# Pinning the making of convolution weights and the stores of zeros to the steps that call them

## The chip, the core and the metric

One NeuronCore of a Trainium2 chip runs the whole program; the other seven are not used. The metric is device time in microseconds for one execution, over a batch of 8 images of 256 channels and 64 x 64 pixels, all in float32. Five engines work side by side, each through a queue of its own: TensorE (PE, matrix products into PSUM), VectorE (DVE), ScalarE (ACT), GpSimd (POOL) and SyncE (SP), which here issues every DMA of the program. Engines wait for each other through semaphores.

## The reference

Two layers follow each other. Cut to what matters:

```python
# layer 0: attention with a reduced set of keys
xr = layernorm_over_channels(conv(x, w_sr, stride=4))        # 16 x 16 positions
q, (k, v) = w_q @ x, split(w_kv @ xr)                        # 8 heads of 32
x = x + gamma_s * (w_out @ (softmax(q @ k.T / sqrt(32)) @ v))
# layer 1: linear attention over two scales
qkv = w_qkv @ x                                              # 768 channels
agg = grouped_1x1(depthwise_5x5(qkv, w_dw), w_pw)            # groups of 8
ms  = concat([qkv, agg])                                     # heads of 8: relu(q), relu(k), v
att = relu_q @ (relu_k.T @ [v, 1]);  att = att[:-1] / (att[-1] + 1e-15)
out = x + batchnorm(w_proj @ att)
```

The kernel multiplies the depthwise 5 x 5 filter and the grouped 1 x 1 filter into one set of weights, so that `agg` becomes a product on TensorE. Making these combined weights is work that depends on no image.

## The kernel before, in words

The program has three passes, one after the other. (A fourth function, `general`, stands behind a test at the end and is not run on these inputs.) Between the passes the data go through scratch memory in HBM.

**First pass** (`first_pass`). Layer 0 and the first projection of layer 1. The main loop runs over n = 0 to 256 + 15. Each n is one step: image b = n // 32, and within the image a strip of 512 pixels (8), a half of the channels (2) and a half of the keys (2). A step issues four products of scores (L784) into PSUM banks, four exponentials on ScalarE (L790), and for the step before it the values (`valued`, L808). At every second step the sums are added on GpSimd (`joined`, L819), the denominators are made (`counted`, L824), and VectorE turns and inverts them (`normed`: L836, L837, L839, L841). Every fourth step, n mod 4 = 2, the output projection (`added`, L856) and the residual sum on VectorE (L857) end a strip, and SP stores it (L860). After every second strip `differences` (L871 to L874) prepares a 2 x 2 scheme of seven products for q, k and v (`qkv`), and these 21 products (L900) are given out over the next seven steps. VectorE and ScalarE empty their banks (L913, L916, L962, L969, L973, L982), and VectorE turns the results (L920) for the stores into `planes` (L933), `k` (L943) and `v` (L948). Scores, projections and products share five PSUM banks in turn. In steps 12 to 19 of an image the strided convolution for the next image runs (`keys_values`, L697), for which SP loads the weights `wsr` (L694) in four buffers; its layer norm follows in steps 20 to 23.

Two jobs without a deadline of their own run beside this loop:

- `conv_weights`, a generator over four parts j = 2, 3, 0, 1 with eight pieces each. It loads `wd` (L668), adds (L670), and for each piece multiplies two broadcast operands on VectorE into `wb` (L674) and stores `wb` to HBM (`wt`, L680). `wd` and `wb` have one buffer each, so a product waits until the store of the product before it has landed. The loop takes one piece per call:

```python
if n > 32 and n % 8 in (3, 6):
    next(weights, None)
if n < n_all:
    b, at = n // 32, n % 32
    if at == (20 if b == 0 else 2):
        border(b)
```

- `border`, which fills the rim of the padded `v` of one image with zeros from the tile `nil`: four stores for each image (L661, L662).

What is written in the loop at some n does not have to run there. The layer that builds the program keeps data dependences and then orders each engine's stream by its own estimate of when operands are ready. An instruction with early operands can move far ahead in its engine's stream. `tc.keep_in_program_order(ins)` adds one constraint: `ins` stays behind the instruction of the same engine that was written just before it. It adds no wait.

**Second pass** (`second_pass`). 64 units of (group of channels, head group, image). It loads `wt`, `planes`, `k` and `v`, makes the combined convolution on TensorE (`convolve`, L1231 and L1235), sums keys with values (L1257, L1274), applies the sums to the queries (`applied`, L1348) and stores attention outputs to `att` (`stored`, called for unit r - 1 in a loop that runs to r = 63, and for the last unit behind the loop). Its constants `taps`, `mix`, `msk`, `rep_w`, `pix` and `ones` are loaded or filled as early as memory of the first pass is free.

**Third pass** (`third_pass`). Reads `att` and `planes`, applies the sums, projects (L1585), normalises and adds the residual.

Of the kernel before, what the change touches and what calls it, by code (L numbers as in the profile page):

```python
# [29 lines left out]
ALU = mybir.AluOpType  # L30
AX = mybir.AxisListType

P = 128
# [5 lines left out]
NB2 = 2 * NB  # L39
NK = NB * NB  # L40
HEADS = 8
D0 = C // HEADS
D1 = 8
# [531 lines left out]
def first_pass(ctx: ExitStack, tc: tile.TileContext, a, fine, planes, x2d, kd, vd, wtd):  # L575
    nc = tc.nc
# [21 lines left out]
    consts, x_tiles = {}, {}  # L598
# [58 lines left out]
    def border(b):  # L657
        v = vd[b].rearrange("n y x e -> y x n e")
        src = nil.rearrange("p (n e) -> p n e", n=8)
        for i in (0, NB2 + 1):  # L660
            nc.sync.dma_start(v[i], src)  # L661
            nc.sync.dma_start(v[1 : NB2 + 1, i], src[:NB2])  # L662


    def conv_weights():
        for j in (2, 3, 0, 1):
            wd = made.tile([P, 16, 6, 16], F32, tag="wd", name=f"wd_{j}", bufs=1)
            nc.sync.dma_start(wd[:, :, :4], a.w_big[:, j].rearrange("p g (n f) -> p g n f", n=4))  # L668

            nc.vector.tensor_add(wd[:, :, 4:], wd[:, :, 0:4:2], wd[:, :, 1:4:2])  # L670
            for i in range(8):
                w = made.tile([P, 2, 6 * 16, D1], F32, tag="wb", name=f"wb_{j}_{i}", bufs=1)
                gs = slice(2 * i, 2 * i + 2)
                nc.vector.tensor_tensor(  # L674
                    w,
                    wd[:, gs].rearrange("p g n f -> p g (n f)").unsqueeze(3).to_broadcast([P, 2, 6 * 16, D1]),
                    consts["wsmall"][:, j, gs].unsqueeze(2).to_broadcast([P, 2, 6 * 16, D1]),
                    ALU.mult,
                )
                nc.sync.dma_start(wtd[j][:, gs], w.rearrange("p g n o -> p g (n o)"))  # L680
                yield
# [309 lines left out]


    weights = conv_weights()
    new_x(0)
    ahead = keys_values(0)
# [29 lines left out]
    n_all = len(order)  # L1025
    todo = {}
    for n in range(n_all + 16):
        m = n - 1
        if n < n_all:
            b, s, c, kc = order[n]  # L1030
# [24 lines left out]
        if n >= 6 and (n - 6) % 4 == 0 and (n - 6) // 4 < B * NG:  # L1055
            b, s = (n - 6) // 4 // NG, (n - 6) // 4 % NG
# [11 lines left out]
# [4 lines that stand above are left out]
            if b + 1 < B:  # L1072
                if at == 10 and b > 0:
                    load_x(b + 1)
                if at == 12:
                    ahead = keys_values(b + 1)
                if 12 <= at < 20:
                    next(ahead)
                    next(ahead)
                elif at >= 20:  # L1080
                    next(ahead, None)
# [20 lines left out]
def second_pass(ctx: ExitStack, tc: tile.TileContext, a, planes, kd, vd, wtd, kvd, attd):  # L1102
    nc = tc.nc
# [21 lines left out]
    n_all = len(units)  # L1125
# [76 lines left out]
    kts, reds, raws, mraws, state, few, qs, bds, done = {}, {}, {}, {}, {}, {}, {}, {}, {}  # L1202
# [161 lines left out]
    def stored(u, par):  # L1364
        t, k, b = units[u]
        c0 = P * t + D0 * k
        tc.keep_in_program_order(
            nc.sync.dma_start(attd[b][c0 : c0 + D0, par].rearrange("c j n -> j c n"), done.pop((u, par)))
        )

    positive(0)
    paired(0, 1)
    for u in range(n_all + 3):
        p, q, r = u - 1, u - 2, u - 3
# [9 lines left out]
        if r > 0:  # L1384
            stored(r - 1, 0)
            stored(r - 1, 1)
# [37 lines left out]
        if now and u + B < n_all:  # L1424
            b = units[u][2]
            load_weights(u + B - b, 1 if b < 4 else 0, b % 4)
    stored(n_all - 1, 0)
    stored(n_all - 1, 1)

# [350 lines left out]
```

## Time and profile before

| | us |
|---|---|
| median of 3 runs (3954.38 to 3956.75) | 3954.98 |
| the profiled execution | 3955.74 |
| its span, first to last instruction | 3954.0 |
| granted TensorE clock over the span | 0.991 |
| VectorE busy in each of the images 2 to 6 of the first pass, which take 248.2 each | 142.5 to 142.8 |

The page gives busy shares over the whole span. The kernel's three passes have different limits: up to some 2010 us the first pass, up to some 3297 us the second, then the third. The forty slices show them as steps in weight loads and GpSimd:

```profile
PEld 4433434435344343443346888888888885555555
DVE  2567565564655646556674566666666664444443
POOL 2334343343433434334433344444444440000000
PEclk9999999999999999999999999999999999999999
DMA  7655544353543534444549887878878757777774
```

Each digit is a tenth of a slice of 99 us. TensorE loads weights for most of the second pass, GpSimd is silent in the third, and DMA engines are busiest in the first two slices and in the second pass. SP issues all transfers in one queue; the ones that the change touches are these (count, size each):

```profile
wt<-wb SPq DMA_DIRECT2D x32, 768.0 KB
...
v<-nil SPq DMA_DIRECT2D x16, 136.0 KB
v<-nil SPq DMA_DIRECT2D x16, 128.0 KB
wd<-in_w_big_dram SPq DMA_DIRECT2D x4, 512.0 KB
```

### The profile page before, as it was taken

Reading aid. Unit: us, or ns where it says so; the run is one execution under the profiler, and the core shown is the slowest. Engines: PE = TensorE matmul, PEld = TensorE weight load, DVE = VectorE, ACT = ScalarE, POOL = GpSimd, SP = SyncE. Lnnn points to the kernel's source line nnn. Section 1 sums busy time; section 2 is a strip of 40 time slices with the busy share of each in tenths; the row PEclk is TensorE's granted clock in tenths of the full one; section 3 lists DMA queues with packets and bytes.
Section 4 is the critical chain, followed back from the end, with each engine's and each line's share of the span. In section 5 each row is a group of like instructions: output and inputs, shape, how many; then the busy total and the mean of one; then the engine's idle time right before and its main releaser. Section 6 shows DMA issues by size and latency. Waiting matters only on the chain. (4 is left out here: it accounts for less than half of the span.)

```text
span 3954.0 us, 70041 instructions
## 1 busy us (share of the span) xinstructions
PE 3873.1 (98%) x27074; PEld 2276.1 (58%) x27074; DVE 2266.0 (57%) x3752; ACT 1516.9 (38%) x3473; POOL 1300.0 (33%) x1394
## 2 busy tenths in 40 slices
PE   8999999999999999999998999999999998999998
PEld 4433434435344343443346888888888885555555
DVE  2567565564655646556674566666666664444443
ACT  3344344443444434444432222222222223554444
POOL 2334343343433434334433344444444440000000
PEclk9999999999999999999999999999999999999999
DMA  7655544353543534444549887878878757777774
GB/s 233 198 152 173 161 137 127 95 155 102 138 129 96 153 100 133 132 117 116 135 116 267 245 233 221 231 223 226 229 214 231 208 145 193 224 210 223 205 227 141
DMA packets 570039, 691.35 MB, mean 175 GB/s; under 512 B 60128, under 2 KB 429280, under 8 KB 565600
## 3 DMA queue, kind: packets, MB, share of 16 engines
q1 hardware_dynamic: 569696, 686.78, 61.2%
q8 instruction: 215, 3.52, 0.4%
q14 instruction: 128, 1.05, 0.1%
HBM read 412.54 MB, written 274.10 MB: 174 GB/s over the span
## 5 line engine op out<-in xcount | busy, mean ns | idle before, releaser
L819 POOL TENSOR_TENSOR e<-e,e 128x512 f32<-128x512 f32 x512 | 685.0, 1369 | 925.7 <-PE av L808 873.2
L790 ACT ACTIVATE e<-sc 128x512 f32<-128x512 f32 x1024 | 530.3, 602 | 801.4 <-PE sc L784 794.4
L1231 PE MATMUL cv<-w,c 128*128 128x128 f32 x3072 | 387.7, 280 | 5.6 <-POOL c L1171 5.1
L1231 PEld LDWEIGHTS cv<-w,c 128*128 128x128 f32 x3072 | 361.2, 193 | 36.2 <-issue 29.3
L784 PE MATMUL sc<-q,kk 32*128 32x512 f32 x2048 | 316.7, 640 | 6.5 <-DVE whole L916 4.8
L1603 DVE TENSOR_TENSOR y<-z,xs 128x256 f32<-128x256 f32 x256 | 141.9, 638 | 310.8 <-ACT z L1594 287.3
L900 PE MATMUL qkv<-differences,combined 128*128 128x512 f32 x576 | 306.2, 623 | 0.4 <-DVE differences L872 0.2
L1274 PE MATMUL sums<-vq,r 128*32 128x288 f32 x4096 | 304.9, 410 | 0.8 <-issue 0.7
L1248 ACT ACTIVATE r<-s 128x512 f32<-128x512 f32 x256 | 160.9, 629 | 316.7 <-DVE s L1247 311.7
L808 PE MATMUL av<-e,vv 128*32 128x512 f32 x2048 | 275.3, 610 | 3.1 <-ACT att L828 3.1
L916 DVE TENSOR_TENSOR whole<-part,qkv 128x512 f32<-128x512 f32 x256 | 175.3, 687 | 178.6 <-PE qkv L900 166.9
L1594 ACT ACTIVATE z<-p,bn 128x256 f32<-128x256 f32 x256 | 133.6, 577 | 313.1 <-PE p L1585 207.4
L1235 PE MATMUL cv<-c,w 128*128 128x128 f32 x2048 | 253.3, 277 | 0.0
L1585 PE MATMUL p<-att,wproj 128*128 128x512 f32 x512 | 249.4, 609 | 1.2 <-ACT att L1568 1.2
L769 PE MATMUL q<-x,wq 128*128 128x512 f32 x512 | 244.3, 599 | 0.0
L1585 PE MATMUL p<-agg,wproj 128*128 128x512 f32 x512 | 240.6, 592 | 0.0
L697 PE MATMUL sr<-x,wsr 128*128 128x256 f32 x1024 | 232.7, 381 | 8.1 <-DMA wsr<-in_w_sr_dram 8.1
L1235 PEld LDWEIGHTS cv<-c,w 128*128 128x128 f32 x2048 | 239.7, 192 | 0.0
L856 PE MATMUL o<-att,wout 128*128 128x512 f32 x512 | 232.8, 596 | 6.2 <-DVE att L841 6.2
L697 PEld LDWEIGHTS sr<-x,wsr 128*128 128x128 f32 x1024 | 195.4, 191 | 59.7 <-issue 26.8
L1238 ACT COPY both<-cv 128x512 f32<-128x512 f32 x128 | 74.9, 585 | 402.9 <-PE cv L1231 351.0
L1247 DVE TENSOR_TENSOR s<-cv,both 128x512 f32<-128x512 f32 x256 | 171.8, 672 | 87.2 <-PE cv L1235 45.5
(143 smaller groups left out, 6029.7 us busy)
## 6 DMA issues: line engine op xcount, KB each, us to landing
vq<-v SPq DMA_DIRECT2D x256, 384.0 KB
planes<-stage SPq DMA_DIRECT2D x128, 578.0 KB
d<-planes SPq DMA_DIRECT2D x128, 578.0 KB
raw<-planes SPq DMA_DIRECT2D x128, 272.0 KB
x<-in_xp_dram SPq DMA_DIRECT2D x64, 512.0 KB
wsr<-in_w_sr_dram SPq DMA_DIRECT2D x128, 256.0 KB
x<-x SPq DMA_DIRECT2D x128, 256.0 KB
k<-turned SPq DMA_DIRECT2D x256, 128.0 KB
```

The costliest lines, as they stand in the source:

```text
L697: nc.tensor.matmul(ps[:, oc], w[:, ci, oc * P : (oc + 1) * P], strips(b, f // 2)[:, ci, f % 2 * NK : (f % 2 + 1) * NK], start=(f == ci == ...
L769: nc.tensor.matmul(ps, consts["wq"][:, ci, c * P : (c + 1) * P], strips(b, s)[:, ci], start=(ci == 0), stop=(ci == 1),)
L784: nc.tensor.matmul(scs[h], kks[b][rows, c, kc * P : (kc + 1) * P], qs[rows], start=True, stop=True)
L790: nc.scalar.activation(e, scs[h], AF.Exp, scale=D0**-0.5)
L808: nc.tensor.matmul(sums["av"][cols], vvs[b][:, kc, c * P + h * D0 : c * P + (h + 1) * D0], es[h], start=(kc == 0), stop=(kc == 1),)
L819: nc.gpsimd.tensor_tensor(es1[h], es0[h], es1[h], ALU.add)
L856: nc.tensor.matmul(ps, consts["wout"][:, c, oc * P : (oc + 1) * P], att[c], start=(c == 0), stop=(c == 1))
L900: nc.tensor.matmul(ps, w, x, start=True, stop=True)
L1231: nc.tensor.matmul(out, x, m, start=(da == 0), stop=(da == 1))
L1235: nc.tensor.matmul(out, m, x, start=(da == 0), stop=(da == 1))
L1274: nc.tensor.matmul(ps[h * D0 : (h + 1) * D0, : 36 * D1].rearrange("p (r n e) -> p r n e", r=3, e=D1), kt[:, par, h, 2 * r + c], vq[:, r : ...
L1585: nc.tensor.matmul(ps.rearrange("p (f q n) -> p f q n", f=4, q=4), wproj[:, j, oc * P : (oc + 1) * P], src, start=(j == 0), stop=(j == 3),)
```

## The change

Three places get or lose the constraint of program order. The two stores of `border` get it on SP. The sum for `wd` and the products for `wb` get it on VectorE; their loads and stores stay free. The stores of attention outputs, which all had it, lose it for the last three units.

```diff
@@ border
         for i in (0, NB2 + 1):
-            nc.sync.dma_start(v[i], src)
-            nc.sync.dma_start(v[1 : NB2 + 1, i], src[:NB2])
+            tc.keep_in_program_order(nc.sync.dma_start(v[i], src))
+            tc.keep_in_program_order(nc.sync.dma_start(v[1 : NB2 + 1, i], src[:NB2]))
@@ conv_weights
-            nc.vector.tensor_add(wd[:, :, 4:], wd[:, :, 0:4:2], wd[:, :, 1:4:2])
+            tc.keep_in_program_order(nc.vector.tensor_add(wd[:, :, 4:], wd[:, :, 0:4:2], wd[:, :, 1:4:2]))
             for i in range(8):
...
-                nc.vector.tensor_tensor(
-                    w,
...
-                    ALU.mult,
+                tc.keep_in_program_order(
+                    nc.vector.tensor_tensor(
+                        w,
...
+                        ALU.mult,
+                    )
                 )
                 nc.sync.dma_start(wtd[j][:, gs], w.rearrange("p g n o -> p g (n o)"))
                 yield
@@ stored
-        tc.keep_in_program_order(
-            nc.sync.dma_start(attd[b][c0 : c0 + D0, par].rearrange("c j n -> j c n"), done.pop((u, par)))
-        )
+        put = nc.sync.dma_start(attd[b][c0 : c0 + D0, par].rearrange("c j n -> j c n"), done.pop((u, par)))
+
+        if u < n_all - 3:
+            tc.keep_in_program_order(put)
```

No operation is added or removed, and no operand changes.

More of the change, by code (lines that the diff above doesn't have):

```diff
@@ L673, in conv_weights @@
                 gs = slice(2 * i, 2 * i + 2)
-                nc.vector.tensor_tensor(
-                    w,
-                    wd[:, gs].rearrange("p g n f -> p g (n f)").unsqueeze(3).to_broadcast([P, 2, 6 * 16, D1]),
-                    consts["wsmall"][:, j, gs].unsqueeze(2).to_broadcast([P, 2, 6 * 16, D1]),
-                    ALU.mult,
+                tc.keep_in_program_order(
+                    nc.vector.tensor_tensor(
+                        w,
+                        wd[:, gs].rearrange("p g n f -> p g (n f)").unsqueeze(3).to_broadcast([P, 2, 6 * 16, D1]),
+                        consts["wsmall"][:, j, gs].unsqueeze(2).to_broadcast([P, 2, 6 * 16, D1]),
+                        ALU.mult,
+                    )
                 )
```

## The prediction

> **What bounds the kernel now.** I read the page first: span, busy shares, 40 slices.
>
> ```profile
> span 3954.0 us, 70041 instructions
> ...
> PE 3873.1 (98%) x27074; PEld 2276.1 (58%) x27074; DVE 2266.0 (57%) x3752; ACT 1516.9 (38%) x3473; POOL 1300.0 (33%) x1394
> ```
>
> TensorE is busy 98%, so the change, which touches no matrix multiplication, can only win back time in which TensorE stands still or runs at a lower clock. The slices do not show where that is. The busy time by stretches does. I cut the first pass at the first exponential of each image (columns: stretch, length, busy time and count of each engine, clock, DMA share, GB/s; these are images 0 to 3):
>
> ```profile
> 52.20:305.60 253.40, 236.97 (x1020) 95.56 (x1019) 155.27 (x193) 101.62 (x240) 100.97 (x84) 0.96 0.56 170
> 305.60:560.20 254.60, 250.86 (x1100) 103.71 (x1104) 159.28 (x228) 107.42 (x258) 103.20 (x101) 1.00 0.53 154
> 560.20:808.50 248.30, 247.91 (x1102) 103.04 (x1104) 142.73 (x217) 106.72 (x259) 95.28 (x101) 1.00 0.45 123
> 808.50:1056.70 248.20, 247.81 (x1100) 102.92 (x1100) 142.54 (x217) 106.63 (x259) 95.33 (x101) 1.00 0.45 124
> ```
>
> Images 2 to 6 take 248.2 us each and TensorE is idle for 0.4 of them. Image 1 takes 6.3 more for the same work. Image 0 takes 253.4 with fewer multiplications (it has no q/k/v products of an earlier image), with 16.4 us idle and a clock of 0.96. Next, who works in images 0 and 1 and not later: the tile `wb`, the second pass's weights.
>
> ```profile
> L674 DVE TENSOR_TENSOR wb<-wd,wsmall x32: 1708/1758/2831, 68.5 to 433.1; 128x1536 f32<-128x1536 f32 x32
> L680 SPq DMA_DIRECT2D wt<-wb x32: 319/344/2193, 71.3 to 458.8; - x32
> its engine sat idle before it (us, times) until:
>   DMA wt<-wb: 42.5, 18
> ```
>
> All 32 products stand between 68.5 and 433.1 us, and 18 times VectorE, which takes its queue in order, sat (42.5 us in all) until the store of the one buffer `wb` had landed. What this does to TensorE shows in the timeline of VectorE around 100 us, and in TensorE's beside it (start, length, ..., in brackets the idle time before and its releaser):
>
> ```profile
> 96.63 1.76 DVE L674 TENSOR_TENSOR wb<-wd,wsmall 128x1536 f32<-128x1536 f32 x1 [1.07 <-DMA wt<-wb]
> 102.51 1.76 DVE L674 TENSOR_TENSOR wb<-wd,wsmall 128x1536 f32<-128x1536 f32 x1 [4.12 <-DMA wt<-wb]
> 104.18 0.71 DVE L836 STREAM_TRANSPOSE rden<-den 128x512 f32<-128x512 f32 x1
> ...
> 106.03 1.13 DVE L841 TENSOR_TENSOR att<-att,rall 128x512 f32<-128x512 f32 x1
> ```
> ```profile
> 101.77 1.02 PE L856 MATMUL o<-att,wout 128*128 128x512 f32 x2
> 107.21 4.54 PE L856 MATMUL o<-att,wout 128*128 128x512 f32 x6 [4.42 <-DVE att L841]
> ```
>
> The denominators end at 97.9 on TensorE; their transpose (L836) starts at 104.2 only, behind a product that waited 4.12 us for a store. TensorE idles 4.42 us, and its next six records take 4.54 us where the same six took 2.84 at 80 us.
>
> [...]
>
> **Part 1: the 32 products and 4 sums go from images 0 and 1 to images 1 to 4.** Pinned, they stay where the loop calls them: steps 3, 6, 11, 14, 19, 22, 27 and 30 of the 32 steps of an image (n above 32, n mod 8 = 3 or 6), images 1 to 4. The order of the two built programs agrees: TensorE's stream is the same in both, instruction for instruction; VectorE's 36 operations move, with a few transposes and ScalarE's `wide` around them; the stores L680 and loads L668 follow on SP.
>
> What goes away. From the timeline I took the start of each step's first exponential (L790) and compared step lengths with the same step of image 3. They agree to 0.1 us in images 2 to 6, so an excess in images 0 and 1 is a loss:
> - image 0, from step 10: 13.9 against 7.5, then 8.6 / 5.0, step 21: 9.2 / 7.4, step 22: 16.3 / 9.2, step 29: 10.4 / 6.5, step 30: 10.6 / 8.3. Sum 25.1.
> - image 0, steps 4 to 9, which lack products, against 4.0 (even, step 4), 4.2 (odd, step 3) and 7.5 with an output projection: 6.4, 8.2, 3.5, 7.4, 4.2 for steps 5 to 9, sum 2.2 + 0.7 - 0.7 + 3.4 + 0 = 5.6.
> - image 1: step 6: 10.8 / 8.3, step 14: 13.4 / 11.8, step 15: 12.1 / 9.9. Sum 6.3.
>
> Together 37.0. Each has a product or its store ahead of it in the queue: at 217 and 221.5 scores wait for `part` and `whole` behind products at 214.1 and 219.1; at 288 the same behind 285.6; at 430 TensorE waits 1.9 us for `wsr`, which SP issues in order behind stores waiting for `wb` (SP waited 71.6 us for L674 before 600 us). A second reading: idle from 52 to 435 us is 20.2 us, and a clock of 0.96 over 253 us is worth 10 more, so 30. I take 37 and keep 30 as the lower end.
>
> What comes. 32 x 1.76 = 56 us and 4 x 0.7 (L670's shortest) = 3 us of VectorE, now in images where it works 142.5 of 248: 15 us an image more, with room. No product waits for its store any more: the nearest two are steps 3 and 6, some 26 us apart, and the store took 3.6 us from product to release at 71 to 74.8. What counts is who stands behind the product. In image 3 the VectorE idle time right behind the eight places is 0.5, 1.4, 0.5, 6.7, 3.0, 3.9, 0.5 and 1.4 us (steps 3 to 30; at steps 19 and 22 a transpose or the tiny `rstd` goes first). The tight place is step 3, 11 or 27; step 27 of image 3:
>
> ```profile
> 1029.64 0.69 DVE L841 TENSOR_TENSOR att<-att,rall 128x512 f32<-128x512 f32 x1
> ...
> 1030.82 0.69 DVE L969 TENSOR_TENSOR part<-part,qkv 128x512 f32<-128x512 f32 x1 [0.48 <-PE qkv L900]
> ...
> 1031.68 0.69 DVE L973 TENSOR_TENSOR part<-part,qkv 128x512 f32<-128x512 f32 x1 [0.17 <-PE qkv L900]
> 1032.34 1.88 PE L769 MATMUL q<-x,wq 128*128 128x512 f32 x4
> 1032.54 0.69 DVE L916 TENSOR_TENSOR whole<-part,qkv 128x512 f32<-128x512 f32 x1 [0.17 <-PE qkv L900]
> ...
> 1034.14 1.14 PE L784 MATMUL sc<-q,kk 32*128 32x512 f32 x8
> ```
>
> The product slips in behind L841 at 1030.3. L969, L973 and L916 empty three of the five product banks, and the scores at 1034.1 take those banks again, the last two at about 1034.7 and 1035.0 (quarters of 1.14 us). At 1.76 us the three end at 1032.8, 1033.5 and 1034.2: 0.8 us to spare, because the query projection (1.88 us) stands between. At 2.83 us[...] they end at 1033.9, 1034.6 and 1035.3: 0.3 us late. So such a place costs 0 to 0.3 us[...]. At step 11 the `sr` products cover more. At steps 6 and 30 the values and denominators (about 2 us) stand before the next scores and the delay is 0.4 to 1.4: nothing. Step 22 delays `rstd`, whose `rs` product comes 6.3 us later (990.6 to 997.1): nothing. Between: half of the 1.76 us products of before (14 or so, such as 164.1, 246.7, 306.2 and 391.2) stood in steps with no loss either. Sum over eight tight places: 0 to 5 us; I take 1.
>
> **Part 2: the 32 stores of zeros** leave 43 to 125 us and go four to an image (step 20 of image 0, step 2 of later ones). Each held SP 0.3 to 5.1 us there. In later images SP is free at that time: after the store at step 2 and the six loads it is idle from 586.0 to 596.4, and four issues at 0.7 us (a median of before) are 3. The x loads behind them serve the next image. One wait is new: the constants `mix`, `msk`, `rep_w`, `pix` and the fill of `ones` come into the zeros' memory, so they now stand in image 7 behind its last stores. The fill, on VectorE at step 3, may wait for four stores issued some 3 us before: 0 to 2 us, once. I take 0.5. The constants are there 200 us ahead of the second pass.
>
> **Part 3: the last six stores of `att` left free.** SP's order at the end is the same in both programs: 0.
>
> Sum: 37.0 - 1.0 - 0.5 = 35.5. The profiled execution took 3955.74 (its span 3954.0 and 1.7 around it); 3955.7 - 35.5 = 3920.2. The median of the runs is 0.8 lower, so 3919.5; I say 3920. With 30 won and 7 given back it is 3932; with 37 and the start freer by a few us, 3915.
>
> **Rivals.**
> - A, the losses up to step 11 of image 0 belong to the start (constants and image 1 loading, GpSimd's L819 waits of up to 1.3 us) and stay. For: 170 GB/s there. Against: the chain above. 37.0 - 15.5 (5.6 + 6.4 + 3.5) - 1.5 = 20 won: 3935.
> - B, places with 0.5 us of idle time cost 1 us each at steps 3, 11, 19 and 27: 16 us back, 3935. Against: the lossless products of before.
> - C, slower: at those 16 steps the product holds the scores' banks, as at step 29 of image 0, which lost 3.9 us. 16 x 3.9 = 62: 3955 - 37 + 62 = 3980. It decides from 2.3 us a place. Against: in step 29 two products and a wait for a store came together, and no store is waited for now.
> - D, SP's new stores at steps 11 and 14 delay `wsr` (1.9 us at 430) twice an image in four images, 15 us, on top of A: 3950. Against: the loads for step 16 were issued at 919, their step starts at 935. That the change leaves the order as it was is ruled out by the built programs.
>
> **How the numbers follow.** Forecast 0.69, A 0.12, B 0.09, C 0.06, D 0.04. 0.2% is 7.9 us, about what a measurement tells from no change. Faster: 0.69 + 0.12 + 0.09, less 0.02 for their tails, 0.88; same 0.05; slower 0.07. The range takes in the forecast's own 3915 to 3932, and A and B: 3912 to 3937.
>
> **What would show it.** Right: image 0 at about 223 us (253.4 - 30.7), image 1 at 248 to 249, images 2 to 4 within 1 us of 248.2, no wait of `wb` for `wt`, second and third pass unchanged in length. Wrong: image 0 still long without products (A); images 1 to 4 longer by 4 (B) or more than 9 (C) with scores waiting for L916 or L973; `sr` waiting for `wsr` (D).

## The result and the profile after

| us | before | after |
|---|---|---|
| median, 16 runs each | 3955.78 (3951.15 to 3961.69) | 3945.74 (3940.05 to 3951.54) |
| profiled execution | 3955.74 | 3944.89 |
| granted clock over the span | 0.991 | 0.992 |

The ratio is 0.9976, 95% interval 0.9968 to 0.9983: about 10 us faster, not the 35 of the forecast. The first lines of the page of the kernel after:

```profile
span 3943.1 us, 70035 instructions
...
PE 3879.8 (98%) x27074; PEld 2282.3 (58%) x27074; DVE 2274.5 (58%) x3752; ACT 1514.9 (38%) x3473; POOL 1294.7 (33%) x1394
```

TensorE is busy 6.7 us longer than before, with the same 27074 multiplications. So something lengthens multiplications. The busy time by stretches, cut again at the first exponential of each image (images 1 to 5, and image 0 in the last line; columns as in the prediction), shows where:

```profile
276.10:529.90 253.80, 253.31 (x1100) 104.97 (x1102) 160.48 (x226) 106.81 (x258) 100.34 (x101) 0.99 0.52 149
529.90:785.40 255.50, 255.02 (x1104) 105.42 (x1103) 160.51 (x226) 106.80 (x258) 100.26 (x101) 0.99 0.52 149
785.40:1039.20 253.80, 253.32 (x1104) 105.05 (x1102) 161.70 (x226) 106.81 (x258) 100.27 (x101) 0.99 0.52 150
1039.20:1291.40 252.20, 251.71 (x1104) 104.49 (x1104) 161.75 (x226) 106.90 (x258) 101.77 (x101) 1.00 0.51 149
1291.40:1539.70 248.30, 247.90 (x1100) 103.07 (x1104) 142.93 (x217) 106.72 (x259) 95.25 (x101) 1.00 0.46 128
53.90:276.10 222.20, 221.42 (x1016) 91.64 (x1018) 108.64 (x167) 100.95 (x241) 86.34 (x84) 1.00 0.32 89
```

Image 0 takes 222.2 us where it took 253.4, and 16 us of idle TensorE are down to 0.8. That part came as forecast. Images 1 to 4, which now make the weights, take 253.8, 255.5, 253.8 and 252.2 instead of 248.2, though TensorE is "busy" for all but 0.5 us of each. Image 5, without products, takes 248.3.

Which steps? I compared each step's length with the same step of an image without products. In images 1 to 4 all steps agree to 0.1 us except two. Step 5, which follows the products and the sum at step 3, is 4.5, 6.1, 4.4 and 2.8 us longer (17.8 in all). Step 29, which follows the product at step 27, is 1.1 to 1.2 longer in each of the four (4.6 in all). In image 7 step 5 is 1.8 longer. That is 24 us given back, of a gross gain of 37.5 (31.2 in image 0, 6.3 in image 1). Step 5 of images 1 to 4, and of image 5 as a measure:

```profile
308.50:319.50 11.00, 11.00 (x42) 3.59 (x45) 6.97 (x11) 4.56 (x9) 1.52 (x2) 0.84 1.03 340
562.30:574.90 12.60, 12.60 (x42) 4.04 (x46) 6.92 (x11) 4.50 (x9) 1.58 (x2) 0.73 1.01 336
817.80:828.70 10.90, 10.90 (x42) 3.67 (x46) 6.92 (x11) 4.50 (x9) 1.58 (x2) 0.84 1.03 359
1071.50:1080.80 9.30, 9.30 (x42) 3.16 (x46) 6.93 (x11) 4.55 (x9) 1.69 (x2) 1.00 1.01 349
1323.70:1330.20 6.50, 6.50 (x36) 2.09 (x40) 4.84 (x8) 4.19 (x9) 0.00 (x0) 1.00 0.99 347
```

The stretch reads 100% busy each time, and the clock is 0.84, 0.73, 0.84 and 1.00. In image 4 the clock is whole, so its 2.8 us are the bare stall; the other three pay 1.7 to 3.4 more at the lower clock. Narrower stretches show how long the clock was low (image 4's stall, in the last line, for comparison):

```profile
311.44:314.85 3.41, 3.41 (x5) 1.33 (x4) 1.81 (x3) 0.78 (x2) 0.00 (x0) 0.50 1.04 397
564.03:570.85 6.82, 6.82 (x10) 2.24 (x9) 2.39 (x4) 1.70 (x3) 0.00 (x0) 0.50 1.02 353
820.03:823.44 3.41, 3.41 (x5) 1.36 (x5) 0.79 (x2) 1.36 (x3) 0.00 (x0) 0.50 0.97 334
1069.20:1076.02 6.82, 6.74 (x16) 2.30 (x15) 5.05 (x7) 3.48 (x6) 3.99 (x3) 1.00 0.64 199
```

TensorE's clock was at half for 3.4, 6.8 and 3.4 us. Half of that, 1.7, 3.4 and 1.7 us, is what images 1 to 3 pay beyond the 2.8 of image 4.

What TensorE waits for shows in the timeline of all engines of the kernel after, image 2. (Line numbers are 2 higher than before: L971, L975 and L918 are the old L969, L973 and L916, the sum is L670, the product L675, GpSimd's addition L821.)

```profile
556.41 0.69 DVE L843 TENSOR_TENSOR att<-att,rall 128x512 f32<-128x512 f32 x1
...
556.68 7.20 POOL L821 TENSOR_TENSOR e<-e,e 128x512 f32<-128x512 f32 x4 [3.52 <-PE av L810]
...
557.02 1.76 DVE L670 TENSOR_TENSOR wd<-wd 128x512 f32<-128x512 f32 x1
...
558.82 2.71 DVE L675 TENSOR_TENSOR wb<-wd,wsmall 128x1536 f32<-128x1536 f32 x1
...
560.97 0.29 PEld L786 LDWEIGHTS sc<-q,kk 32*128 32x128 f32 x2 [0.76 <-issue]
560.97 4.64 PE L786 MATMUL sc<-q,kk 32*128 32x512 f32 x8
...
561.45 0.67 DVE L971 TENSOR_TENSOR part<-part,qkv 128x512 f32<-128x512 f32 x1
...
562.17 0.29 PEld L786 LDWEIGHTS sc<-q,kk 32*128 32x128 f32 x2 [0.91 <-DVE part L971]
...
562.22 0.69 DVE L975 TENSOR_TENSOR part<-part,qkv 128x512 f32<-128x512 f32 x1
...
562.96 0.29 PEld L786 LDWEIGHTS sc<-q,kk 32*128 32x128 f32 x2 [0.50 <-DVE part L975]
563.01 0.69 DVE L918 TENSOR_TENSOR whole<-part,qkv 128x512 f32<-128x512 f32 x1
...
563.76 0.29 PEld L786 LDWEIGHTS sc<-q,kk 32*128 32x128 f32 x2 [0.50 <-DVE whole L918]
```

Sum and product stand one behind the other: 4.4 us of VectorE between L843 and L971. The scores' first pair starts at 560.97; each later pair wants a bank that L971, L975 or L918 is still to empty, and they empty one each 0.8 us. The last pair is 2.79 us behind the first, which is the bare stall of image 4. On the PE row the eight records are one run of 4.64 us, "busy" (1.14 at the place that the prediction shows). Only the PEld row, the weight loads, has the waits in brackets. The list of all waits of the weight loads, 300 to 1320 us, agrees (columns: total us, times, longest):

```profile
PEld sc L786 <- DVE whole L918: 8.3, 16, 0.7
PEld sc L786 <- DVE part L971: 3.6, 4, 0.9
PEld sc L786 <- DVE part L975: 2.0, 4, 0.5
```

Before had neither the second line nor the third, and 5.2 us in 10 waits in place of the first. The four waits each for L971 and L975 are step 5 of images 1 to 4 and nowhere else.

### The profile page after: what moved, and what is told of

Read it like the earlier page. It is cut to its first block, busy times and chain, and to the rows that moved or that the text cites. A ratio compares the mean times of both kernels' runs of the same rounds, so it can differ in the third digit from the quotient of the medians.

```text
span 3943.1 us, 70035 instructions
## 1 busy us (share of the span) xinstructions
PE 3879.8 (98%) x27074; PEld 2282.3 (58%) x27074; DVE 2274.5 (58%) x3752; ACT 1514.9 (38%) x3473; POOL 1294.7 (33%) x1394
## 5 line engine op out<-in xcount | busy, mean ns | idle before, releaser
L821 POOL TENSOR_TENSOR e<-e,e 128x512 f32<-128x512 f32 x512 | 684.0, 1367 | 906.9 <-PE av L810 872.5
L1233 PEld LDWEIGHTS cv<-w,c 128*128 128x128 f32 x3072 | 361.6, 193 | 35.6 <-issue 29.3
L918 DVE TENSOR_TENSOR whole<-part,qkv 128x512 f32<-128x512 f32 x256 | 175.7, 688 | 196.1 <-PE qkv L902 183.7
```

The source lines that it names most:

```text
L821: nc.gpsimd.tensor_tensor(es1[h], es0[h], es1[h], ALU.add)
L1233: nc.tensor.matmul(out, x, m, start=(da == 0), stop=(da == 1))
```

## The experiments

Theory: the loss is the queue at step 3 (sum and product ahead of the three operations that empty the scores' banks), and to a smaller part at step 27. Rivals: the pinned stores of zeros, which load the DMA queues at steps 2 to 5 of each image, and a price of the products themselves wherever they stand. Each run is compared with runs of the kernel before on the same chip; "excess" is a step's length less that of the same step without products.

**Weights alone.** The stores of zeros stay free as they were before; the rest is as in the kernel after.

```diff
-            tc.keep_in_program_order(nc.sync.dma_start(v[i], src))
-            tc.keep_in_program_order(nc.sync.dma_start(v[1 : NB2 + 1, i], src[:NB2]))
+            nc.sync.dma_start(v[i], src)
+            nc.sync.dma_start(v[1 : NB2 + 1, i], src[:NB2])
```

> The weights (sum and products) pinned, the stores of zeros free as before, the last stores of attention as in the changed kernel. Theory (the sum and the first product of a part stand together before L971 at step 3 and hold the banks of the scores): step 5 of images 1 to 4 keeps its excess of 2.8 to 6.1 us, step 29 its 1.2; the excess of 1.8 us in image 7 goes, since no store of zeros is late there; time within 4 us of the changed kernel, some 10 us faster than before. Rival (the stores of zeros and the loads queued behind them on SP cause step 5): the excess at step 5 goes, and the time falls by some 18 us below the changed kernel.

Measured: 3945.06 us (3941.17 to 3947.59, 15 runs), ratio 0.9977 (0.9969 to 0.9985). Step 5 exceeds by 4.5, 6.1, 4.4 and 2.8 us, to the tenth what the kernel after shows; step 29 by 1.2. Image 7 loses nothing. So the zeros take no part in the losses of images 1 to 4; their whole price by the steps is the 1.8 us in image 7, too little to show between the two medians.

**Zeros alone.** The kernel before with only those two stores pinned.

> The stores of zeros pinned, weights free as before. Theory: images 0 and 1 lose 31 to 37 us as before, step 5 of images 2 to 4 has no excess, image 7 loses 1.8 us at step 5 behind the fill of ones: time 0 to 4 us above before. Rival (the zeros' stores cause step 5): step 5 of images 1 to 4 shows 3 to 6 us: some 18 us above before.

Measured: 3956.14 us (3951.77 to 3963.44, 13 runs), ratio 1.0006 (0.9998 to 1.0014). Images 0 and 1 keep their losses (252.2 and 258.1 us, where the kernel before has 253.4 and 254.6; the profiled execution, with 3963.44, was the longest of the 13), no step 5 or 29 exceeds, and image 7 has its 1.8 us. So the gain is not from clearing the zeros out of image 0, and the rival falls on both sides. The 1.8 us is VectorE's fill of the constant `ones`, written into the memory of `nil` and so behind its last stores. VectorE in image 7 of the kernel after:

```profile
1814.38 0.69 DVE L843 TENSOR_TENSOR att<-att,rall 128x512 f32<-128x512 f32 x1
1818.38 0.06 DVE L1200 MEMSET ones<- 128x1 f32 x1 [3.31 <-DMA v<-nil]
1818.38 0.69 DVE L971 TENSOR_TENSOR part<-part,qkv 128x512 f32<-128x512 f32 x1
```

A fill of 0.06 us holds VectorE for 3.31, because the last store of `nil` had been issued from 1812.49 on; L971 is late again.

**The sum two steps earlier.** The sum gets a call of its own, at step 1.

```diff
             tc.keep_in_program_order(nc.vector.tensor_add(wd[:, :, 4:], ...))
+            yield
...
-        if n > 32 and n % 8 in (3, 6):
+        if n > 32 and (n % 8 in (3, 6) or n % 32 == 1):
```

> As the changed kernel, but the four sums L670 are called two steps earlier, at step 1, so that at step 3 a product stands alone, as at step 27. Theory: the excess of step 5 falls from 2.8 to 6.1 us to about the 1.2 us of step 29, four times, and no new excess comes at steps 1 to 3; time about 13 us below the changed kernel, 23 below before (3932). Rival (the first product itself, or its place, costs it): step 5 keeps 2.8 us or more, time within 4 us of the changed kernel.

Measured: 3932.59 us (3929.61 to 3933.53, 5 runs), ratio 0.9945 (0.9932 to 0.9959). Step 5 exceeds by 1.1 to 1.2 us in each of the four images: step 3, now with a product alone, costs what step 27 costs. The waits of scores for L971 and L975 are gone. At step 3 of image 1 VectorE's product takes 2.82 us, and of the four pairs of scores one still waits:

```profile
304.81 0.67 PEld L787 LDWEIGHTS sc<-q,kk 32*128 32x128 f32 x6 [0.76 <-issue]
305.98 0.29 PEld L787 LDWEIGHTS sc<-q,kk 32*128 32x128 f32 x2 [0.50 <-DVE whole L919]
```

The last pair starts 1.17 us behind the first, and that is the step's 1.1 to 1.2; undisturbed, all eight loads come in one run of 0.31 us (before, image 3, at 1034.14). Some loss came elsewhere: 3.5 instead of 1.8 in image 7 and 0.8 at step 7 of image 3.

**GpSimd silent beside the products.** At steps 4 and 28 of images 1 to 4 the addition L821, which runs beside sum and product, is left out, so those denominators count half of the keys.

```diff
-                joined(es.pop(m - 1), es[m])
+                if n // 32 in (1, 2, 3, 4) and n % 32 in (4, 28):
+                    es.pop(m - 1)
+                else:
+                    joined(es.pop(m - 1), es[m])
```

> As the changed kernel, but the four sums on GpSimd (L821) at steps 4 and 28 of images 1 to 4 are left out, so that those denominators count half of the keys. Theory[...]: the sum falls from 1.76 to about 0.7 us and the product at these places from 2.7 or 2.8 to 1.75; L971 comes 2 us earlier at step 3 and 1.1 earlier at step 27; the excess of step 5 falls to 0 to 1, that of step 29 to 0. Rival (the durations belong to the operands, not to GpSimd): both stay, and so do the excesses.

Measured: 3926.60 us (2 runs), ratio 0.9932 (0.9914 to 0.9950). Step 5 exceeds by 0.8 in each of the four images, step 29 by nothing (and, as with the sum moved, step 7 of image 3 by 0.8). Sum and product in the two kernels, first after, then this one (tile `wd`: shortest, median, longest in ns; then the timeline of this one):

```profile
L670 DVE TENSOR_TENSOR wd<-wd x4: 1753/1758/1759, 303.2 to 1066.3; 128x512 f32<-128x512 f32 x4
```
```profile
L670 DVE TENSOR_TENSOR wd<-wd x4: 684/684/684, 303.3 to 1051.6; 128x512 f32<-128x512 f32 x4
```
```profile
303.28 0.68 DVE L670 TENSOR_TENSOR wd<-wd 128x512 f32<-128x512 f32 x1
304.00 1.76 DVE L675 TENSOR_TENSOR wb<-wd,wsmall 128x1536 f32<-128x1536 f32 x1
305.68 0.68 DVE L971 TENSOR_TENSOR part<-part,qkv 128x512 f32<-128x512 f32 x1
...
307.23 1.89 PE L786 MATMUL sc<-q,kk 32*128 32x512 f32 x8
```

Beside GpSimd's addition the sum takes 1.07 us more and the product 0.95 to 1.07 more. The two take 2.4 us at this place, not 4.5; L971 starts 1.5 us ahead of the scores, not 0.5 behind. The run leaves GpSimd's work out, so its total is no offer; it shows who lengthens the queue, and that 2.4 us are still 0.8 too many. (GpSimd's four additions at this place in image 2 of the kernel after take 7.20 us, in image 5, without products, 5.24: GpSimd waits as well.)

**Other places.** The sum at step 11, products at steps 13, 14, 15, 17, 19, 22, 30 and at step 6 of the next image: none at 3 or 27.

```diff
             tc.keep_in_program_order(nc.vector.tensor_add(wd[:, :, 4:], ...))
+            yield
...
-        if n > 32 and n % 8 in (3, 6):
+        if n > 42 and n % 32 in (6, 11, 13, 14, 15, 17, 19, 22, 30):
```

> As the changed kernel, but no work at steps 3 and 27: the sum alone at step 11, the eight products at steps 13, 14, 15, 17, 19, 22 and 30 and at step 6 of the next image. Theory (cost is only where the scores of the next step take banks that the delayed operations must empty, less 0.9 us of slack): no step of images 0 to 5 is longer than the same step without a product by over 0.5 us, but for step 7 where a product meets GpSimd (0.8 at most); image 7 keeps the wait of the fill of ones (1.8 to 3.5). Time 3927 to 3930. Rival (a product costs something wherever it stands): 32 times 0.3 us or more remain, time 3936 or above.

Measured: 3928.53 us (3927.68 to 3930.04, 5 runs), ratio 0.9933 (0.9919 to 0.9946). Steps 5 and 29 exceed by nothing, though as many products run. So a product has no price of its own; its place has. One thing was not foreseen: in each image with products step 18 is 3.5 us shorter and step 19 is 4.3 longer, net 0.8. Eight `sr` multiplications (16 records) stand one step later in TensorE's stream, and there TensorE meets a late load of weights. In image 1 SP issues all eight loads of `wsr` from 424.32 on, behind the store of `x` at 422.05; in the kernel after, four of them go ahead of that store. Why the builder chose this order is not shown.

```profile
427.48 3.72 PE L700 MATMUL sr<-x,wsr 128*128 128x256 f32 x16 [0.56 <-DMA wsr<-in_w_sr_dram]
```

**Other places, and the fill held back.** As the last, and the fill of `ones` pinned too, which puts it behind the first pass.

```diff
-    nc.vector.memset(ones, 1.0)
+    tc.keep_in_program_order(nc.vector.memset(ones, 1.0))
```

> As e5_places, and the fill of ones pinned behind the first pass. Theory: the excess at step 5 of image 7 (1.8 to 3.5 us) goes and nothing comes at the start of the second pass: 2 to 3 us below e5_places, 3924 to 3927. Rival: the fill behind the first pass is late for the first sums of the second and gives the 2 us back there.

Measured: 3925.04 us (3921.23 to 3928.32, 5 runs), ratio 0.9923 (0.9909 to 0.9936). Step 5 of image 7 exceeds by nothing. By the steps that is worth 1.8 us; the medians differ by 3.5, and their ranges overlap, so the size is from the steps. This is the best version measured: 20.7 us below the median of the kernel after, though from another set of runs (29.5 below its own kernel before, where the kernel after is 10.0 below).

**The product at step 27 twice.** The reverse test: a longer queue at a place that cost 1.2.

```diff
+                for _ in range(2 if i == 6 else 1):
-                tc.keep_in_program_order(nc.vector.tensor_tensor(w, ...))
+                    tc.keep_in_program_order(nc.vector.tensor_tensor(w, ...))
```

> As the changed kernel, but the product at step 27 of images 1 to 4 is issued twice in a row. Theory (delay less a fixed slack): L971 comes 2.8 us later or less, so step 29 goes from an excess of 1.2 to 3 to 4 us, and where TensorE's clock falls meanwhile up to 6; time 8 to 16 us above the changed kernel. Rival (step 29's 1.2 us have another cause than the queue behind the product): about 1.2 stays.

Measured: 3968.14 us (3965.27 to 3970.59, 5 runs), ratio 1.0034 (1.0021 to 1.0047). The sign is right, the size missed: step 29 exceeds by 6.6 to 6.7 us in all four images. TensorE there, in image 1:

```profile
504.32 1.12 PE L787 MATMUL sc<-q,kk 32*128 32x512 f32 x2
506.65 3.65 PE L787 MATMUL sc<-q,kk 32*128 32x512 f32 x6 [1.21 <-DVE part L972]
510.23 2.08 PE L903 MATMUL qkv<-differences,combined 128*128 128x512 f32 x2
```

The two records at 510.23 take 2.08 us where the same two take 1.13 at full clock (before, 1035.22). The last pair of scores was 3.9 us behind the first (508.23 less 504.32, by the weight loads); the rest of the 6.6 is the lower clock: at half for 6.83 us from 506.89 (at 512.10 two records still take 1.83, from 513.77 four take 1.88), worth 3.4, of which 0.7 fell into the stall itself. I had allowed for up to 6 where the clock falls, but not for a fall each time: here it fell four times of four. The four are nearly one case (see the clock, below). Step 5, which this edit leaves alone, exceeds by 4.4 to 4.5 us in all four images, with the clock at half for 3.41 us each time, in image 4 too.

Does the sum over steps explain the totals? What each kernel gives back by its steps, beside its median less that of the kernel before in the same set:

| | given back by steps | median less before | gain before giving back |
|---|---|---|---|
| after | 24.1 | -10.0 | 34.1 |
| weights alone | 22.4 | -9.6 | 32.0 |
| sum at step 1 | 13.5 | -22.1 | 35.6 |
| GpSimd silent | 6.1 | -28.1 | 34.2 |
| other places | 5.2 | -26.1 | 31.3 |
| other places, fill held back | 3.8 | -29.5 | 33.3 |
| product twice | 46.1 | +13.6 | 32.5 |

The last column, the sum of the two (the sign turned), stays at 31 to 36 while the middle one moves over 43 us. It is less than the 37.5 read from images 0 and 1. In the profile of the kernel after, the start is 1.6 us longer than before (first exponential at 53.9, not 52.2) and the later passes 0.8, which makes 35.1 of it. These two parts scatter: over the nine profiles the first exponential stands between 51.9 and 54.9 us, and what follows the first exponential of image 7, less the excess of its step 5, takes 2152.6 to 2156.6. The differences within the last column are of that size; their cause is not shown.

## Why the prediction was wrong, step by step

- **What goes away: right.** Forecast 37.0; the steps show 37.5, the totals 31 to 36. Image 0 was to take about 223 us and takes 222.2; image 1 lost its 6.3. Rival A, that the early losses belong to the start, falls: they went with the products, as the run with weights alone shows. (Two readings were loose, and nothing hangs on them: step lengths of images 2 to 6 agree to 0.3 us, not 0.1, and the 3.5 in rival A's sum is 3.6.)
- **What comes: the step that failed.** "0 to 5 us; I take 1" measured 22.4 (17.8 at step 5, 4.6 at step 29). The mechanism was in the text, as "the product holds the scores' banks"; its size was wrong, for four reasons.
  - *Step 3 was taken for a place like step 27.* The sum stands there with the product. I priced the four sums only in VectorE's total and never put sum and product together into that queue. Moving the sum alone took 12 us off (each against its own kernel before: -10.0, then -22.1).
  - *The sum was priced at its shortest, 0.7 us.* It took 1.76 all four times beside GpSimd's additions, and 0.68 in the run with GpSimd silent. The prediction took up to 2.83 us for the product and asked nothing like it of the sum. So the queue at step 3 was 4.47 us, not 1.76 or 2.83. The profile before had this very pair, beside four GpSimd additions (L819, 7.15 us from 66.44 on); 0.7 us was the sum in two other places, where GpSimd was idle:

```profile
66.75 1.75 DVE L670 TENSOR_TENSOR wd<-wd 128x512 f32<-128x512 f32 x1
68.54 2.71 DVE L674 TENSOR_TENSOR wb<-wd,wsmall 128x1536 f32<-128x1536 f32 x1
```

  - *The slack was read too wide.* I let the scores want their last banks at quarters of their 1.14 us, to come out with 0.3 late at 2.83. The view of weight loads before has all eight loads within 0.31 us at 1034.14: the four want their banks together. The third bank was free at 1033.23 without a product (1032.54 + 0.69), so 0.9 us was all the slack, and a product of 2.83 us costs 1.2 at step 29, not 0.3.
  - *The clock.* The prediction's 0 to 5 us left room, by its author's estimate, for a lower clock on 0.3 us a place. On 2.8 us the clock added 1.7, 3.4 and 1.7 in images 1 to 3, nothing in image 4. In the traces of before and after, the clock is at 0.50 in 12 and 11 stretches. Each lasts one, two or three times 3.413 us (the last of each trace is cut off by the end), and within a trace all begin on marks 3.413 us apart: those of images 2 and 3 start 252.59 and 508.59 us after that of image 1, 74 and 149 times 3.413. The four stalls at step 5 of the kernel after are alike, each with waits of 0.91, 0.50 and 0.50 us between running multiplications, but fall differently between such marks. The scores' first weight load came 2.5, 0.4, 3.3 and 1.1 us behind a mark in images 1 to 4, and the clock was at half for one, two, one and none of the 3.413. The stalls being equally long (2.79 us), in these four cases the outcome goes with where a stall fell. In the product twice the four sums start 259.3 us apart on average (301.3 to 1079.2), and 76 times 3.413 is 259.4: if its marks are as far apart, its four stalls fall at nearly one place between them. How much idle time lowers the clock is not shown.
- **The other six places: right.** After the products at steps 6, 11, 14, 19, 22 and 30 no step exceeds, as the idle time behind them said.
- **The fill of `ones`: right in kind, 0.5 forecast, 1.8 measured**, inside its 0 to 2. The fill waited 3.31 us.
- **Stores of zeros, otherwise at nothing: right** (zeros alone, 1.0006). **The freed stores of `att`, at nothing:** not tried alone; SP's order is the same in both programs, and the later passes moved by 0.8 us, inside the 4 us by which they differ between profiles.
- **No product waits for its store: right.** No wait of `wb` for `wt` is left.
- **Rivals.** B was nearest: 16 us at some steps of images 1 to 4. But it spread 1 us over steps 3, 11, 19 and 27; in truth 4.4 of the 5.6 an image are at step 3, and 11 and 19 are free. Rival C put 3.9 us on every one of its places. At step 5 that size came true (2.8 to 6.1). I set it aside because at its model, step 29 of image 0, "two products and a wait for a store came together": two operations come together at step 3 too. D did not show in the kernel after; the run with other places comes near it, where 0.8 us an image go with a late load of `wsr`.

## What to carry to other kernels

When work is pinned to a step, add up everything that the step then issues on that engine, each at the duration that it has beside its neighbours there (here 1.76 us for the sum, not 0.68), and set the sum against the time until the operations queued behind it must have emptied a bank; that is a different question from how idle the engine is. A stall of TensorE on a bank can stand inside one run of "busy" records (here 2.79 us in one of 4.64): compare equal steps, the clock, and the waits of the weight loads, before believing a busy share. Work without a deadline goes behind places whose followers have none either: the same operations cost 22.4 us at steps 3 and 27 and at most about 0.8 an image elsewhere.

## What the runs showed of the hardware

- A VectorE addition of 128x512 float32 took 0.684 us alone and 1.76 beside a run of GpSimd additions; a broadcast product of 128x1536 took 1.75 and 2.43 to 2.83. The extra is neither a fixed price nor a share: in the kernel after, each of the 18 that started while a GpSimd addition (1.27 us undisturbed) was running took longer by what that addition still had to run, less 0.13 to 0.14 us. The product at 558.82 had 1.09 left and took 0.96 more, the one at 1088.65 had 0.82 left and took 0.68 more. Before, 14 such operations took 0 to 1.08 more, within 0.07 us of the same sum. A GpSimd addition that came due meanwhile waited in turn: the third of the four at 556.68 took 2.78.
- With three waits of its weight loads, of 0.91, 0.50 and 0.50 us, TensorE's clock fell in three of four images. It was then at 0.50 for 3.41 or 6.82 us, in stretches that begin on marks 3.413 us apart through the whole trace, and the loss was half of that time: 1.7 or 3.4 us.
- A fill waited 3.31 us, until 1818.38, for stores of zeros whose last issue began at 1812.49.
